# Router scores of tiles 0 to 12 by multiplication on GpSimd and sums on VectorE, in a perceiver block with a mixture of experts

## The chip, the cores and the metric

The kernel runs on one core of a Trainium2 chip. The time is the device time of one launch in microseconds; the figure to compare is the median of several launches. A core has five engines that run side by side, each through its own list of instructions in order: TensorE (PE; its weight loads are listed apart as PEld), VectorE (DVE), ScalarE (ACT), GpSimd (POOL) and SyncE (SP), which here only issues transfers. Where one engine needs what another makes, its instruction waits for a semaphore, and everything behind it on that engine waits too.

## The reference

Three residual stages over x (64 sequences of 32 tokens, 256 wide, all float32). What the change touches is the choice of experts, at the head of the third stage; `Wr` is 8 x 256.

```
x = x + cross_attention(layernorm(x), ctx_512)     # 16 heads of 64, 257 context rows
x = x + self_attention(layernorm(x))               # 4 heads of 64, rotary
x = x + ffn(layernorm(x))

# ffn(x):
scores_BSN = jnp.einsum('bsd,nd->bsn', x, Wr) + br
w_BSN = jax.nn.softmax(scores_BSN, axis=-1)
_, idx_BSK = jax.lax.top_k(scores_BSN + biases_N, 2)
val_BSK = jnp.take_along_axis(w_BSN, idx_BSK, axis=-1)
val_BSK = val_BSK / jnp.sum(val_BSK, axis=-1, keepdims=True)
# each token then goes through its two experts of eight:
# silu(x @ Wl1[:, :512]) * (x @ Wl1[:, 512:]) @ Wl2, weighted by val_BSK
```

## The kernel before

The 2048 tokens are 16 tiles of 128 tokens, and a tile is four sequences of 32. A tile lies with its tokens on the 128 partitions.

**The main loop** goes over the 64 (tile, sequence) pairs. One turn transposes the softmax weights of the present sequence (`tp`, L332), forms the scores of the next sequence in four groups (`s`, L309), and mixes the context (`pa`, L342). Each group of scores gets a maximum on VectorE (`nmx`, L313) and an exponential on ScalarE (L314); after every second group VectorE takes reciprocals (L319) and scales the two groups in place (L321). The scaled weights (`pr`) are what the next turn's `tp` reads. Three PSUM buffers hold the `s` groups.

**Steps in between.** Everything else of a tile is a Python generator that is advanced at six places of a turn, by a table of eight rows: four rows (one for each sequence) for even tiles and four for odd ones. "ahead" advances the queries of later tiles, "near" and "far" the generator `rest` (L528) of the tile before and of the one before that. `rest` runs through output projection, self-attention, a layernorm that writes `xr` (L535), and the router `route` (L470). It has 13 steps: six "near" and, one tile later, seven "far". What is still left of "far" at the end of a tile's fourth row is run off there.

The places of a row are: after the first `tp`; after two score groups; after the second `tp` and the third group; after the fourth group, two places in a row; after the mix. I call the four rows of a tile its first to fourth row.

**The router.** Its first step puts the token number into the last column of `xr` (L472, GpSimd), transposes `xr` in two halves on TensorE (`trr`, L191) and copies the result to SBUF on ScalarE (`xrT`, L192). Its second multiplies with `wr_sb` on TensorE (`pr`, L478, eight columns) and then runs a chain of small VectorE instructions: add the bias (`rsc`, L480), find the two largest (L484 to L488), mark them (`rtwo`, `rboth`, L491 to L495), and form the weights (L497 to L506). Its third counts on TensorE where each token goes in its expert's list (`pk`, L510, from `rboth` and `seen`), forms the slots on VectorE (L513 to L519), and GpSimd scatters `xr` to the list in DRAM (L521, twice). In the trace the PSUM product of the router and the softmax weights of the cross-attention both carry the name `pr`; the line tells them apart.

**Order.** SyncE and TensorE run in the order of the program (`manual_schedule`). VectorE, ScalarE and GpSimd are put in order by the framework's scheduler at compile time; `tc.keep_in_program_order` pins an instruction behind the one that precedes it in the program on its engine.

**Buffers.** The pool `xp` holds, by tags, `xg` (5 buffers: rows gathered for an expert block, and `none`, the zeros that first clear the lists), `y` (4) and `bxT` (2), all used by the expert blocks from tile 15 on. The `xr`, `xaT` and `xrT` tiles have two buffers each in the pool `wk`. PSUM tag `a` has three banks, used by the router's transposition, product and count and by most other products.

**After the loop** the routed tokens go through blocks of 128 for one expert each: six early blocks begin while tiles 14 and 15 finish (L703), the others run with weights streamed in (L732). That part begins at about 640 us.

Of the kernel before, what the change touches and what calls it, by code (L numbers as in the profile page):

```python
# [9 lines left out]
FP = mybir.dt.float32  # L10
U32 = mybir.dt.uint32
AF = mybir.ActivationFunctionType
ALU = mybir.AluOpType
AX = mybir.AxisListType
PSUM = bass.MemoryType.PSUM

P = 128
D = 256
TOK = 2048
NT = TOK // P  # L20
# [9 lines left out]
NE = 8  # L30
# [20 lines left out]
def block_kernel(  # L51
# [13 lines left out]
    awo: bass.AP,  # L65
    abo: bass.AP,
    freq: bass.AP,
    wr_t: bass.AP,
    br: bass.AP,
    bias_n: bass.AP,  # L70
# [4 lines left out]
    nc = tc.nc  # L75
# [19 lines left out]
    def load(dst, src):  # L95
        nc.sync.dma_start(out=dst, in_=src)
# [10 lines left out]
    def pool(name, bufs):  # L107
        return ctx.enter_context(tc.tile_pool(name=name, bufs=bufs))
# [35 lines left out]
    wr_sb = const.tile([P, 2, NE], FP, name="wr_sb")  # L144
    br_bc = const.tile([P, NE], FP, name="br_bc")
# [17 lines left out]
    wk = pool("wk", 2)  # L163
    sm = pool("sm", 4)
    xp = pool("xp", 3)
    tb = pool("tb", 1)

    def bank(shape, name):
        return ps.tile([P] + shape, FP, tag="a", name=name)
# [17 lines left out]
    def transposed(dst, src, n, name):  # L187

        pt = bank([n, P], f"tr{name}")
        for k in range(n):  # L190
            nc.tensor.transpose(pt[:, k, :], src[:, k * P : (k + 1) * P], ident)  # L191
        nc.scalar.copy(dst, pt)  # L192
# [277 lines left out]
    def route(t, xr):  # L470

        nc.gpsimd.tensor_copy(xr[:, RW - 1 : RW], token[:, t : t + 1])  # L472
        xT = wk.tile([P, 2, P], FP, tag="xrT", name=f"xrT{t}")
        transposed(xT, xr, 2, f"r{t}")
        yield
        pr = bank([NE], f"pr{t}")
        for k in range(2):
            nc.tensor.matmul(pr, xT[:, k, :], wr_sb[:, k, :], start=(k == 0), stop=(k == 1))  # L478
        sc = sm.tile([P, NE], FP, tag="rsc", name=f"rsc{t}")
        nc.vector.tensor_tensor(sc, pr, br_bc, ALU.add)  # L480
        sel = sm.tile([P, NE], FP, tag="rsel", name=f"rsel{t}")
        nc.vector.tensor_tensor(sel, sc, bn_bc, ALU.add)
        top = sm.tile([P, 8], FP, tag="rtop", name=f"rtop{t}")
        nc.vector.max(top, sel)  # L484
        idx = sm.tile([P, 8], U32, tag="ridx", name=f"ridx{t}")
        nc.vector.max_index(idx, top, sel)
        idf = sm.tile([P, 2, 1], FP, tag="ridf", name=f"ridf{t}")
        nc.vector.tensor_copy(idf[:, :, 0], idx[:, 0:2])  # L488

        two = sm.tile([P, 2, NE], FP, tag="rtwo", name=f"rtwo{t}")  # L490
        nc.vector.tensor_tensor(  # L491
            two, expert_id2, idf.to_broadcast([P, 2, NE]), ALU.is_equal
        )
        both = sm.tile([P, NE], FP, tag="rboth", name=f"rboth{t}")
        nc.vector.tensor_tensor(both, two[:, 0, :], two[:, 1, :], ALU.add)  # L495
        nmx = sm.tile([P, 1], FP, tag="rnmx", name=f"rnmx{t}")
        nc.vector.tensor_reduce(nmx, sc, AX.X, ALU.max, negate=True)  # L497
        ex = sm.tile([P, NE], FP, tag="rex", name=f"rex{t}")
        nc.scalar.activation(ex, sc, AF.Exp, bias=nmx)
        nc.vector.tensor_tensor(ex, ex, both, ALU.mult)  # L500
        tot = sm.tile([P, 1], FP, tag="rtot", name=f"rtot{t}")
        nc.vector.tensor_reduce(tot, ex, AX.X, ALU.add)
        inv = sm.tile([P, 1], FP, tag="rinv", name=f"rinv{t}")
        nc.vector.reciprocal(inv, tot)
        ew = xr[:, D : D + NE]
        nc.vector.tensor_scalar(ew, ex, inv, None, ALU.mult)  # L506
        yield

        pk = bank([NE], f"pk{t}")
        nc.tensor.matmul(pk, before, both, start=True, stop=False)  # L510
        nc.tensor.matmul(pk, ones, seen, start=False, stop=True)
        at = sm.tile([P, 1, NE], FP, tag="rat", name=f"rat{t}")
        nc.vector.tensor_tensor(at[:, 0, :], pk, region[:, 0, :], ALU.add)  # L513
        nc.vector.tensor_tensor(seen, seen, both, ALU.add)
        nc.vector.tensor_tensor(two, two, at.to_broadcast([P, 2, NE]), ALU.mult)
        slot = sm.tile([P, 2], FP, tag="rslot", name=f"rslot{t}")
        nc.vector.tensor_reduce(slot, two, AX.X, ALU.add)
        slots = sm.tile([P, 2], U32, tag="rslots", name=f"rslots{t}")
        nc.vector.tensor_copy(slots, slot)  # L519
        for k in range(2):  # L520
            nc.gpsimd.indirect_dma_start(  # L521
                out=routed[:, :],
                out_offset=bass.IndirectOffsetOnAxis(ap=slots[:, k : k + 1], axis=0),
                in_=xr,
                in_offset=None,
            )

    def rest(t, cT, lastT, ut):  # L528

        yield from cross_output(t, cT, lastT, ut)  # L530
        xn = normed(t, "s")
        yield
        yield from self_attention(t, xn)
        xr = wk.tile([P, RW], FP, tag="xr", name=f"xr{t}")
        normed(t, "r", xr[:, 0:D])  # L535
        yield
        yield from route(t, xr)
# [265 lines left out]
    def rotary_tables():  # L803
# [72 lines left out]
        ("", "far", "ahead", "near", "far", ""),  # L876
        ("near", "far", "", "near", "far", ""),
        ("ahead", "far", "ahead", "near", "far", "ahead"),
        ("near", "", "ahead", "near", "", "far"),
        ("", "far", "ahead", "near", "far", ""),  # L880
        ("near", "far", "", "near", "far", ""),
        ("ahead", "far", "ahead", "near", "far", "ahead"),
        ("", "", "near", "near", "", "far"),
    )
    kvs, probs = {0: context0}, {}
    seqs = [(t, b) for t in range(NT) for b in range(4)]
# [80 lines left out]
    for n, (t, b) in enumerate(seqs):  # L967
# [31 lines left out]
        pr, pts = probs.pop((t, b)), []  # L999
# [175 lines left out]
```

## Time and profile before

| | us |
|---|---|
| median of 3 launches (809.91 to 810.59) | 810.36 |
| the profiled launch, its own time | 811.05 |
| its span, first to last instruction | 809.3 |
| granted TensorE clock, mean | 0.994 |

Busy time in four stretches of the span, in us:

| stretch | length | PE | DVE | ACT | POOL |
|---|---|---|---|---|---|
| 60 to 100 | 40 | 38.6 | 28.7 | 20.7 | 2.9 |
| 100 to 580 | 480 | 471.5 | 332.4 | 258.3 | 69.1 |
| 580 to 640 | 60 | 55.5 | 39.3 | 25.6 | 17.3 |
| 640 to 809 | 169 | 157.8 | 63.6 | 42.3 | 46.7 |

Rows of the trace that bear on the change (durations of one instruction):

| line, engine | what | shape | ns |
|---|---|---|---|
| L191 PE | `trr`, 2 per tile | 128x128 | 273 |
| L192 ACT | `xrT` copy | 128x256 | 368 |
| L478 PE | `pr`, 4 per tile | 128x8 | 256 |
| L350 POOL | addition of two SBUF tiles | 128x256 | 722 |
| L313 DVE | maximum, from PSUM | 128x257 to 128x1 | 421 |
| L321 DVE | scale, SBUF to SBUF | 128x256 | 350 |
| L497 DVE | maximum, from SBUF | 128x8 to 128x1 | 153 |

How to read it: a page's busy time counts an instruction from start to end, and instructions overlap in an engine's pipe, above all on TensorE; what an instruction costs its engine is better seen from the start of one to the start of the next. An idle time is listed with the instruction that ended it. In a line of the timeline the columns are start, duration, engine, source line, operation, output<-inputs, shapes, count, and in brackets the idle time ahead of it and what released it.

### The profile page before, as it was taken

The page shows a single profiled execution, that of the slowest core. Times are in us where ns is not written, and L with a number is a line of the kernel's source. Part 1 is how long each engine was busy: PE and PEld are TensorE (multiplying, and loading weights), DVE is VectorE, ACT ScalarE, POOL GpSimd, SP SyncE. Part 2 cuts the span into 40 slices and gives each one's busy share as a digit, 9 for nine tenths or more (in the row PEclk, how much of TensorE's full clock was granted, in tenths as well). Part 3 has the DMA queues.
Part 4 walks back from the last instruction along what each step waited for, and adds up shares of the span by engine and source line. Part 5 has one row for each costly group of instructions (what it writes and reads, how often), then busy time and mean ns, then how long its engine had stood idle before and what let it go on. Part 6 is the DMA issues. An engine that isn't in the chain of part 4 may idle for free. (4 is left out here: it accounts for less than half of the span.)

```text
span 809.3 us, 15134 instructions
## 1 busy us (share of the span) xinstructions
PE 778.6 (96%) x5212; PEld 612.5 (76%) x5212; DVE 496.9 (61%) x2045; ACT 378.3 (47%) x1078; POOL 143.7 (18%) x195
## 2 busy tenths in 40 slices
PE   8899999999999999999999999999998999999994
PEld 7576777677767767777767777676677899999994
DVE  4657666766686677677677766768665734334332
ACT  3564555556465555556554555555435322222220
POOL 3001011120201011111101110121123313333332
PEclk9999999999999999999999999999999999999998
DMA  9440202021020202022020102020441495356321
GB/s 306 140 112 1 66 11 67 11 89 51 27 79 11 67 10 80 10 75 65 27 66 11 66 11 67 14 73 15 163 162 34 114 398 144 54 139 210 60 41 21
DMA packets 32735, 64.14 MB, mean 79 GB/s; under 512 B 5328, under 2 KB 23632, under 8 KB 31120
## 3 DMA queue, kind: packets, MB, share of 16 engines
q1 hardware_dynamic: 26128, 54.08, 19.8%
q0 software_dynamic: 6528, 9.06, 6.2%
q8 instruction: 43, 0.70, 0.4%
q14 instruction: 36, 0.29, 0.1%
HBM read 87.54 MB, written 13.16 MB: 124 GB/s over the span
## 5 line engine op out<-in xcount | busy, mean ns | idle before, releaser
L314 ACT ACTIVATE pr<-s,nmx 128x257 f32<-128x257 f32 x256 | 121.7, 479 | 110.1 <-DVE nmx L313 101.9
L313 DVE TENSOR_REDUCE nmx<-s 128x1 f32<-128x257 f32 x256 | 105.8, 421 | 70.3 <-PE s L309 69.7
L309 PE MATMUL s<-kv,q 128*128 128x257 f32 x512 | 142.8, 387 | 1.6 <-ACT pr L314 1.4
L342 PE MATMUL pa<-pt,kv 128*128 128x512 f32 x256 | 123.3, 604 | 5.3 <-ACT ov L366 5.3
L309 PEld LDWEIGHTS s<-kv,q 128*128 128x128 f32 x512 | 89.1, 192 | 16.1 <-ACT pt L336 3.0
L332 PEld LDWEIGHTS tp<-ident,pr 128*128 128x128 f32 x512 | 61.5, 144 | 30.4 <-issue 15.7
L321 DVE TENSOR_SCALAR pr<-pr,inv 128x256 f32<-128x256 f32 x256 | 82.3, 363 | 3.3
L521 POOL DMA_INDIRECT routed<-xr,rslots x32 | 32.9, 1027 | 283.6 <-DVE lastT L1006 215.9
L332 PE MATMUL tp<-ident,pr 128*128 128x128 f32 x512 | 80.2, 278 | 1.6 <-DVE pr L321 1.6
L345 ACT COPY cT<-pa 128x512 f32<-128x512 f32 x64 | 37.5, 585 | 89.3 <-PE pa L342 89.3
L336 ACT COPY pt<-tp 128x512 f32<-128x512 f32 x128 | 75.4, 590 | 6.3 <-PE tp L332 6.0
L342 PEld LDWEIGHTS pa<-pt,kv 128*128 128x128 f32 x256 | 46.1, 190 | 39.8 <-issue 28.3
L695 POOL DMA_INDIRECT out_x<-y_late,to_late x28 | 43.5, 1555 | 107.3 <-DMA out_x<-y_late,to_late 33.5
L285 PE MATMUL pqh<-xqT,xwq_sb 128*128 128x256 f32 x256 | 60.8, 381 | 0.8 <-ACT xqT L192 0.8
L375 PE MATMUL po<-xwo_sb,ov 128*128 128x256 f32 x256 | 60.3, 379 | 0.0
L375 PEld LDWEIGHTS po<-xwo_sb,ov 128*128 128x128 f32 x256 | 48.6, 190 | 6.6
L285 PEld LDWEIGHTS pqh<-xqT,xwq_sb 128*128 128x128 f32 x256 | 47.4, 190 | 7.9 <-ACT xqT L192 1.5
L314 ACT ACTIVATION_READ_ACCUMULATOR pr<-s,nmx 128x1 f32 x256 | 51.7, 202 | 0.0
L319 DVE RECIPROCAL inv<-sums 128x2 f32<-128x2 f32 x128 | 20.5, 160 | 44.3 <-ACT pr L314 44.0
L631 ACT COPY bxT_late<-pxT_late 128x256 f32<-128x256 f32 x28 | 10.4, 372 | 73.1 <-PE pxT_late L629 73.1
L390 PE MATMUL pqkv<-awqkv_sb,xaT 128*128 128x512 f32 (+1 forms) x128 | 43.9, 486 | 0.0
L350 POOL TENSOR_TENSOR xb<-x,xbo_bc 128x256 f32<-128x256 f32 x16 | 11.6, 726 | 165.8 <-issue 117.2
(259 smaller groups left out, 1284.0 us busy)
## 6 DMA issues: line engine op xcount, KB each, us to landing
lane<-in_wall SPq DMA_DIRECT2D x24, 1028.0 KB
lane<-in_wall SPq DMA_DIRECT2D x24, 640.0 KB
lane2a<-in_wall SPq DMA_DIRECT2D x10, 1028.0 KB
kv<-in_ctx_t SPq DMA_DIRECT2D x16, 514.0 KB
kv<-in_ctx_a SPq DMA_DIRECT2D x16, 512.0 KB
lane2b<-in_wall SPq DMA_DIRECT2D x10, 640.0 KB
xg_late<-routed SPq DMA_DIRECT2D x28, 132.5 KB
x<-in_x SPq DMA_DIRECT2D x16, 128.0 KB
```

The costliest lines, as they stand in the source:

```text
L285: nc.tensor.matmul(pq[:, mm, :], xwq_sb[:, k, m * P : (m + 1) * P], xqT[:, k, :], start=(k == 0), stop=(k == 1),)
L309: nc.tensor.matmul(s, qb[:, g * P : (g + 1) * P], kvT[:, b, :], start=True, stop=True)
L313: nc.vector.tensor_reduce(nmx, s, AX.X, ALU.max, negate=True)
L314: nc.scalar.activation(pr[:, g, :], s, AF.Exp, bias=nmx, accum_out=sums[:, g : g + 1])
L321: nc.vector.tensor_scalar(pr[:, i, :ML], pr[:, i, :ML], inv[:, i : i + 1], None, ALU.mult)
L332: nc.tensor.transpose(tp[:, g * P : (g + 1) * P], pr[:, g, j * P : (j + 1) * P], ident)
L336: nc.scalar.copy(pt, tp)
L342: nc.tensor.matmul(pa, kvA[:, b, j, :], pts[j], start=(j == 0), stop=(j == MC - 1))
L345: nc.scalar.copy(cT[:, :, b, :], pa.rearrange("p (h n) -> p h n", n=SEQ))
L375: nc.tensor.matmul(po, ov[:, m, :], xwo_sb[:, m, :], start=False, stop=(m == XH // 2 - 1))
L390: nc.tensor.matmul(pq, xaT[:, k, :], awqkv_sb[:, k, lo:hi], start=(k == 0), stop=(k == 1))
L695: nc.gpsimd.indirect_dma_start(out=out[:, :], out_offset=bass.IndirectOffsetOnAxis(ap=self.to[:, b : b + 1], axis=0), in_=y, in_offset=Non ...
```

## The change

For tiles 0 to 12 (`t < NT - 3`) the router no longer uses TensorE for the scores. The eight rows of `Wr` are loaded once at the start, each spread over all 128 partitions (`wr_rows`; 128 KB each, eight transfers on SyncE's queue behind the other constants). They lie in buffers of the tags `y` and `bxT`, which the expert blocks need only later, and in two new ones. For each expert GpSimd multiplies `xr` with the expert's row, and VectorE sums the product over its 256 columns. This goes in two halves of four experts with a step's end between: the first "far" step issues four products, the second four sums and the next four products, the third the other four sums and the chain from `rsc` on. The sums are pinned in program order; the products use the five `xg` buffers. The router thus has one more step (14 in `rest`), and the two rows of the table that had only one "far" get a second.

Tiles 13, 14 and 15 keep transposition and product; their `xrT` now shares the buffers of the tag `xaT`.

```diff
+    wr_rows = []
+    for e in range(NE):
+        tag, bufs = (("y", 4), ("bxT", 2), ("gates_wr", 2))[(e > 3) + (e > 5)]
+        wr_rows.append(xp.tile([P, D], FP, tag=tag, bufs=bufs, name=f"wr_row{e}"))
+        load(wr_rows[e], wr[e, :].partition_broadcast(P))
...
     def route(t, xr):
 
         nc.gpsimd.tensor_copy(xr[:, RW - 1 : RW], token[:, t : t + 1])
-        xT = wk.tile([P, 2, P], FP, tag="xrT", name=f"xrT{t}")
-        transposed(xT, xr, 2, f"r{t}")
-        yield
-        pr = bank([NE], f"pr{t}")
-        for k in range(2):
-            nc.tensor.matmul(pr, xT[:, k, :], wr_sb[:, k, :], start=(k == 0), stop=(k == 1))
         sc = sm.tile([P, NE], FP, tag="rsc", name=f"rsc{t}")
-        nc.vector.tensor_tensor(sc, pr, br_bc, ALU.add)
+        if t < NT - 3:
+
+            sums = sm.tile([P, NE], FP, tag="rsums", name=f"rsums{t}")
+            for half in range(2):
+                four = range(NE // 2 * half, NE // 2 * (half + 1))
+                prods = {}
+                for e in four:
+                    prods[e] = xp.tile([P, D], FP, tag="xg", bufs=5, name=f"rprod{t}_{e}")
+                    nc.gpsimd.tensor_tensor(prods[e], xr[:, 0:D], wr_rows[e], ALU.mult)
+                yield
+                for e in four:
+                    tc.keep_in_program_order(
+                        nc.vector.tensor_reduce(sums[:, e : e + 1], prods[e], AX.X, ALU.add)
+                    )
+            nc.vector.tensor_tensor(sc, sums, br_bc, ALU.add)
+        else:
+            xT = wk.tile([P, 2, P], FP, tag="xaT", name=f"xrT{t}")
+            transposed(xT, xr, 2, f"r{t}")
+            yield
...
+            nc.vector.tensor_tensor(sc, pr, br_bc, ALU.add)
...
-        ("near", "", "ahead", "near", "", "far"),
+        ("near", "far", "ahead", "near", "", "far"),
...
-        ("", "", "near", "near", "", "far"),
+        ("", "far", "near", "near", "", "far"),
```

More of the change, by code (lines that the diff above doesn't have):

```diff
@@ L67, in block_kernel @@
     freq: bass.AP,
+    wr: bass.AP,
     wr_t: bass.AP,
@@ L472, in route @@
         nc.gpsimd.tensor_copy(xr[:, RW - 1 : RW], token[:, t : t + 1])
-        xT = wk.tile([P, 2, P], FP, tag="xrT", name=f"xrT{t}")
-        transposed(xT, xr, 2, f"r{t}")
-        yield
-        pr = bank([NE], f"pr{t}")
-        for k in range(2):
-            nc.tensor.matmul(pr, xT[:, k, :], wr_sb[:, k, :], start=(k == 0), stop=(k == 1))
-        sc = sm.tile([P, NE], FP, tag="rsc", name=f"rsc{t}")
-        nc.vector.tensor_tensor(sc, pr, br_bc, ALU.add)
+        sc = sm.tile([P, NE], FP, tag="rsc", name=f"rsc{t}")
+        if t < NT - 3:
[16 more added lines that the diff above has]
+            yield
+            pr = bank([NE], f"pr{t}")
+            for k in range(2):
+                nc.tensor.matmul(
+                    pr, xT[:, k, :], wr_sb[:, k, :], start=(k == 0), stop=(k == 1)
+                )
+            nc.vector.tensor_tensor(sc, pr, br_bc, ALU.add)
         sel = sm.tile([P, NE], FP, tag="rsel", name=f"rsel{t}")
@@ L1150 @@
         "freq": a["L0_attn_nrope_freq"],
+        "wr": a["L0_ffn_Wr"],
         "wr_t": a["L0_ffn_Wr"].T,
```

## The prediction

> **What bounds the kernel now.** I read the busy rows and the forty slices first, then what TensorE waits for in the steady part (100 to 580 us), then the timeline around one router, and last the busy time of each row of steps.
>
> ```profile
> PE 778.6 (96%) x5212; PEld 612.5 (76%) x5212; DVE 496.9 (61%) x2045; ACT 378.3 (47%) x1078; POOL 143.7 (18%) x195
> ...
> PE   8899999999999999999999999999998999999994
> DVE  4657666766686677677677766768665734334332
> ```
>
> TensorE is the bound: 9 in nearly every slice, while VectorE stands at 6 to 7 and GpSimd, in its own row, at 0 to 2 until the last third. In the steady part TensorE's waits, by releaser (us in all, times, longest), are small:
>
> ```profile
> PE pa L342 <- ACT ov L366: 4.9, 13, 0.4
> PE trr L191 <- DVE xr L184: 1.6, 2, 0.8
> ```
>
> With two more of 1.0 us each (the second is pr <- q, five times 0.2) that is 8.5 us in 480. So work taken off TensorE is time gained, as long as no new wait arises; and TensorE runs in order, so each new wait is lost whole. The question is how much router work goes, and how late VectorE becomes.
>
> **What goes from TensorE.** An even tile (start and duration in us; "trr" is the router's transposition, "pr" its product):
>
> ```profile
> 182.63 0.38 PE L191 MATMUL trr<-ident,xr 128*128 128x128 f32 x2
> 182.85 0.60 PE L332 MATMUL tp<-ident,pr 128*128 128x128 f32 x4
> ...
> 186.10 0.51 PE L478 MATMUL pr<-wr_sb,xrT 128*128 128x8 f32 x4
> 186.47 1.96 PE L342 MATMUL pa<-pt,kv 128*128 128x512 f32 x4
> ```
>
> Matmuls overlap, so I go from start to start: 182.63 to 182.85 is 0.22 us, 186.10 to 186.47 is 0.37, together 0.59. In the odd tile after it, trr takes 220.24 to 220.46, 0.22, and pr 223.61 to 224.07, 0.46, with 0.20 of idle before it (for a VectorE copy that frees its bank): 0.88. Thirteen routers change (tiles 0 to 12, seven even, six odd): 7 x 0.59 + 6 x 0.88 = 9.4 us. If nothing else moved, the median of 810.4 would become 801.0. ScalarE also loses a copy (L192, 0.37) per tile, 4.8 us in all, off the path.
>
> **What is added.** Eight products per tile on GpSimd. The nearest row is L350, the same shape from two SBUF tiles: 0.72, and two back to back 1.46, so 0.73 each, 5.8 us a tile, 76 us in all. GpSimd goes from 143.7 to about 220 us, 27%. The first four can start when xr is there (181.87) and end by 184.9; their sums are issued behind the row's last scores, about 188. A fifth fits the free buffer; the other three wait for one sum each and end near 191, before the second four sums can begin (195). Behind them in GpSimd's order stand the two scatters, which before left only at 201.3. No wait from there, if no product is longer than 1.2 us.
>
> Eight sums on VectorE, 128x256 from SBUF; none is in the trace. Below: two reductions over 257 elements from PSUM together in 0.75 (220.38), 0.33 from start to start. Above: 0.43, the same pair fed one by one (0.86). Four sums are then 3 x 0.33 + 0.42 = 1.41 us, at most 1.72. I take 1.41, as all four inputs are ready. Over 13 tiles 37 to 45 us.
>
> Eight loads of 128 KB at the start, each of one row given to all partitions: SyncE's issue of the like xbo_bc took 0.43, so 3.5 to 4 us behind bn_bc (18.72). What slides is the zeroing of the scatter buffer, and the second context, issued at 26.0 and first read near 50: 20 us of cover, cost nothing.
>
> The other shapes are free: one more "far" step in each second half-table keeps pace with one more yield (14 steps in place of 13). The last three routers only change the name of a buffer.
>
> **Where it meets the path: the fourth row of steps.** The scores used to be done in the third row (rsc at 186.65), and both picks (rboth, 188.46 + 0.12 = 188.58) lay nine microseconds ahead of pk, which counts them on TensorE. Now the second four sums stand in the fourth row, pinned behind the scale of its first two score groups, and everything from rsc to rboth follows them. What that scale and pk stand at today:
>
> ```profile
> 195.39 0.62 DVE L321 TENSOR_SCALAR pr<-pr,inv 128x256 f32<-128x256 f32 x2
> ...
> 197.86 0.62 DVE L321 TENSOR_SCALAR pr<-pr,inv 128x256 f32<-128x256 f32 x2
> 198.12 0.28 PE L510 MATMUL pk<-rboth,before 128*128 128x8 f32 x2
> ...
> 198.48 0.63 PE L332 MATMUL tp<-ident,pr 128*128 128x128 f32 x4
> ```
>
> The last scale ends at 198.48, just when tp, which reads it, starts: there is no slack here. On this clock less 0.59: the pin opens at 196.01 - 0.59 = 195.42; four sums to 196.83; rsc to rboth took 1.93 with a scale pair (0.61) in between, so 1.32: 198.15. pk is due at 198.12 - 0.59 = 197.53: late 0.62, and 0.42 more if the last maximum (nmx, 196.60) goes in between: 1.04. Behind pk on TensorE stand the next sequence's tp and all that follows; behind the sums on VectorE that nmx, and ScalarE's exponential waits for it. The scale: with nmx after the sums at 196.83 in place of 196.60 - 0.59 = 196.01, plus some of the small instructions, 0.8 to 1.1 late. I take 0.95, less 0.59 gained: +0.36 per even tile.
>
> The odd fourth row is 7.3 us long. VectorE's busy time there and in the even one (columns: span, then PE, PEld, DVE):
>
> ```profile
> 189.40:198.40 9.00, 9.00 (x42) 6.49 (x41) 5.36 (x17) 4.34 (x13) 0.00 (x0) 1.00 0.00 1
> 227.00:234.30 7.30, 7.30 (x34) 4.99 (x33) 5.45 (x18) 3.77 (x12) 0.00 (x0) 1.00 0.00 0
> ```
>
> To 5.45 come 1.41 of sums and some 1.6 of router: 8.5 in 7.3. About 1.2 of rotary and mask work can slide into the next row, but that one has 7.33 of 9.00 already. From the pin (230.62) to the scale's end (234.36) VectorE is idle for 1.0 today, and 2.4 comes in (1.41, and eight small ones at about 0.13 net): 1.4 late, less 0.88: +0.5. Sum: 7 x 0.36 + 6 x 0.5 = 5.5 us. The rotary behind (L401 to L405) is then up to 0.1 late for its transposition: 1.3. Together +6, so 816 for the median. (The profiled run was 811.05, its span 809.3, and 1.75 lies around it; I add to the median.)
>
> **The shared port.** GpSimd's products hold up the scales:
>
> ```profile
> 18.94 1.46 POOL L350 TENSOR_TENSOR xb<-x,xbo_bc 128x256 f32<-128x256 f32 x2 [10.27 <-DMA xbo_bc<-in_xbo]
> ...
> 19.40 1.15 DVE L321 TENSOR_SCALAR pr<-pr,inv 128x256 f32<-128x256 f32 x2
> ```
>
> Under two GpSimd additions the pair took 1.15, elsewhere 0.62: 0.53 lost. One or two pairs a tile meet products, 0.5 to 1.1 us, in the third row, where the last scale ends at 188.21 and tp starts at 189.43: 1.2 of cover, and the router's small work has left. So 0; without the cover 13 x 0.53 = 7 us. The Trainium skill, "SBUF — State Buffer", section "Who interferes with whom", says that GpSimd and a VectorE instruction in a two-port mode hold one port pair in turn, whole instructions long, and that a tensor_reduce never takes it. The row agrees for the scales; by the rule the sums are not slowed, and if they were, by 0.5 for each four, the sum would be 13 us worse. "GPSIMD Engine Reference", section 4.1, advises against elementwise work there as about twice as slow; here 0.72 against VectorE's 0.42, hidden as long as GpSimd has nothing urgent.
>
> **Rivals.** (1) The backlog: as above, 816; own range 811 to 822; 0.42. (2) VectorE hides it: the scores would have to start 1 us earlier than the pin allows today, by ScalarE doing the second exponential of the row before the copy of pt (0.57) that stands ahead of it, and small work yielding to the scales. Speaking for it: VectorE would be only 67% busy. All hidden gives 801, half (0.5 a tile) 807; 0.36. (3) VectorE's fixed order puts sums and router behind the fourth row's last scale (197.89): rboth at 197.89 + 1.41 + 1.32 = 200.6, pk 3.1 late, less 0.59, 2.5 a tile, 33 us: 843; for half the tiles 827. It decides where the compiler believes the products later than they are; against it, they end some 4 us earlier; 0.14. (4) Gain and wait cancel, or the freed 0.7 reappears as another wait: 810; 0.08.
>
> **The numbers.** Within 0.2%, 1.6 us, is about what a measurement tells from no change. Faster 0.36 (case 2), same 0.08, slower 0.56 (1 and 3). Range 801 (all hidden) to 827 (case 3 in half the tiles).
>
> **What would show it.** pk and the next tp waiting for rboth or pr, 0.5 to 1.1 us in each changed tile, right; no such wait and a total near 801, wrong. Sums at 0.33 from start to start, products at 0.73. Wrong too if products end later than their sums are due, or if the third row, not the fourth, holds the new wait.

## The result, and the profile after

The changed kernel takes 828.11 us (median of 5, 827.2 to 828.72) beside 809.91 before (median of 5, 808.56 to 810.59): a ratio of 1.0226, 95% interval 1.0212 to 1.024, so 18.2 us slower. The profiled launch took 828.05, its span 826.3.

The busy row of the page and the group of the products (busy us and mean ns of one, then the idle time ahead of them and what ended it), of the changed kernel:

```profile
PE 776.8 (94%) x5134; PEld 603.7 (73%) x5134; DVE 531.3 (64%) x2149; ACT 373.9 (45%) x1065; POOL 217.6 (26%) x299
...
L490 POOL TENSOR_TENSOR rprod<-xr,wr_row 128x256 f32<-128x256 f32 x104 | 73.5, 739 | 37.3 <-DVE rsums L494 34.2
```

TensorE has 1.8 us less to do by this count, VectorE 34 more, GpSimd 74 more. TensorE's waits in its steady part (100 to 595 us) show where the time went:

```profile
PE pk L536 <- DVE rboth L521: 12.9, 13, 3.1
PE pa L350 <- DVE q L285: 6.5, 6, 1.2
```

Both are new: 12.9 us before pk, in all thirteen changed tiles, and 6.5 us in six places where the context product waits for VectorE's copy of q (before, the longest wait for this copy was 0.2). Both come from VectorE being late.

**Row by row.** The kernel repeats the same work, so the loss can be located. I take the start of each sequence's first `pa` from TensorE's timeline and measure from one to the next. B runs from a tile's first row to its second, C from the second to the third, D from the third to the fourth, E from the fourth to the next tile's first. C holds the router's old work on TensorE, E holds pk and the next tp. Means over four even and four odd tiles (tiles 4 to 11), in us; starts are read to 0.01, so a mean can be off by as much:

| | even B | C | D | E | odd B | C | D | E |
|---|---|---|---|---|---|---|---|---|
| before | 9.92 | 8.59 | 9.93 | 9.17 | 9.92 | 8.58 | 8.21 | 8.35 |
| after, less before | 0.00 | -0.59 | -0.07 | +1.66 | 0.00 | +0.29 | +0.02 | +0.86 |

Tile 14, in which the router of tile 12 runs, stands apart: C, D and E are -0.47, +0.60 and +5.39. From the first `pa` of the loop to the last one it is 18.6 us more, which is the whole loss. What comes ahead of the loop and behind it is not longer, and the eight new loads cost nothing that shows: of two kernels among the experiments below, t11, which has them, comes to its first `pa` at 27.7 us, and sums_only, which has not, at 27.9.

The even E, in the timeline of the changed kernel (the two sums of four are one line, x4):

```profile
195.35 0.62 DVE L329 TENSOR_SCALAR pr<-pr,inv 128x256 f32<-128x256 f32 x2
...
195.88 1.39 DVE L494 TENSOR_REDUCE rsums<-rprod 128x1 f32<-128x256 f32 x4
...
197.19 0.41 DVE L321 TENSOR_REDUCE nmx<-s 128x1 f32<-128x257 f32 x1
...
197.52 0.16 DVE L496 TENSOR_TENSOR rsc<-rsums,br_bc 128x8 f32<-128x8 f32 x1
...
198.46 0.35 DVE L329 TENSOR_SCALAR pr<-pr,inv 128x256 f32<-128x256 f32 x1
...
198.81 0.35 DVE L329 TENSOR_SCALAR pr<-pr,inv 128x256 f32<-128x256 f32 x1
199.08 0.16 DVE L521 TENSOR_TENSOR rboth<-rtwo 128x8 f32<-128x8 f32 x1
...
199.29 0.39 PE L536 MATMUL pk<-rboth,before 128*128 128x8 f32 x2 [1.06 <-DVE rboth L521]
...
199.76 0.63 PE L340 MATMUL tp<-ident,pr 128*128 128x128 f32 x4
```

The pin opens at 195.9, the four sums end at 197.3, the last maximum goes ahead of rsc, and the reciprocal and both scales go between rsc and rboth. pk waits 1.06 us on TensorE's row until 199.29, and the last scale ends at 199.16, so that tp could not have run much earlier either.

The odd C:

```profile
221.55 3.57 POOL L490 TENSOR_TENSOR rprod<-xr,wr_row 128x256 f32<-128x256 f32 x5
...
224.18 1.10 DVE L329 TENSOR_SCALAR pr<-pr,inv 128x256 f32<-128x256 f32 x2
...
225.20 0.68 DVE L285 COPY q<-pq 128x512 f32<-128x512 f32 x1
...
225.93 1.98 PE L350 MATMUL pa<-pt,kv 128*128 128x512 f32 x4 [1.18 <-DVE q L285]
```

Five products run on GpSimd from 221.55 to 225.12. The pair of scales at 224.18 takes 1.10 in place of 0.61; the copy of q behind it ends at 225.88 and `pa`, which takes the bank that this copy frees, waits 1.18 us.

The end of tile 14:

```profile
566.08 1.39 DVE L494 TENSOR_REDUCE rsums<-rprod 128x1 f32<-128x256 f32 x4
...
567.50 0.17 DVE L496 TENSOR_TENSOR rsc<-rsums,br_bc 128x8 f32<-128x8 f32 x1
...
569.59 0.16 DVE L521 TENSOR_TENSOR rboth<-rtwo 128x8 f32<-128x8 f32 x1
...
569.80 0.60 PE L536 MATMUL pk<-rboth,before 128*128 128x8 f32 x2 [3.11 <-DVE rboth L521]
...
571.23 0.59 PE L572 MATMUL pc_early<-seen,ones 128*128 128x8 f32 x2 [0.40 <-DVE seen L540]
```

Here rsc to rboth takes 2.2 us, as the rotary instructions go in between, pk waits 3.11 us and the count for the early blocks follows at once. From the row's first `pa` to pk it is 4.99 us, 3.28 more than before. Behind pk lies a second loss: from 569.5 to 576.4 us the granted TensorE clock was 0.51. The same four transpositions behind the count, in the changed kernel and in chain_late, an experiment below that also waits 0.40 for the count:

```profile
571.67 1.09 PE L340 MATMUL tp<-ident,pr 128*128 128x128 f32 x4
```
```profile
561.63 0.63 PE L332 MATMUL tp<-ident,pr 128*128 128x128 f32 x4
```

From pk to the next `pa` the changed kernel takes 9.99 us, chain_late 7.25. So some 2.7 us of this row are the lower clock, an estimate from these two kernels. The loop of the kernel before has no such stretch.

### The profile page after: what moved, and what is told of

The parts are those of the page before. It is cut to its first block, busy times and chain, and to the rows that moved or that the text cites. A ratio compares the mean times of both kernels' runs of the same rounds, so it can differ in the third digit from the quotient of the medians.

```text
span 826.3 us, 15143 instructions
## 1 busy us (share of the span) xinstructions
PE 776.8 (94%) x5134; PEld 603.7 (73%) x5134; DVE 531.3 (64%) x2149; ACT 373.9 (45%) x1065; POOL 217.6 (26%) x299
## 5 line engine op out<-in xcount | busy, mean ns | idle before, releaser
L329 DVE TENSOR_SCALAR pr<-pr,inv 128x256 f32<-128x256 f32 x256 | 89.6, 388 | 3.7
L490 POOL TENSOR_TENSOR rprod<-xr,wr_row 128x256 f32<-128x256 f32 x104 | 73.5, 739 | 37.3 <-DVE rsums L494 34.2
L350 PEld LDWEIGHTS pa<-pt,kv 128*128 128x128 f32 x256 | 46.0, 190 | 47.9 <-issue 27.1
```

Of the source, the lines that this page charges most:

```text
L329: nc.vector.tensor_scalar(pr[:, i, :ML], pr[:, i, :ML], inv[:, i : i + 1], None, ALU.mult)
L350: nc.tensor.matmul(pa, kvA[:, b, j, :], pts[j], start=(j == 0), stop=(j == MC - 1))
L490: nc.gpsimd.tensor_tensor(prods[e], xr[:, 0:D], wr_rows[e], ALU.mult)
```

## The experiments

My theory was that VectorE is late in two places, each by its own cause: in the fourth row by the sums and the chain, in the odd third row by GpSimd's products. The rivals put all of it on one of these parts, on pk's place, or on the order of the PSUM banks; what theory 1, 2 or 3 stands for in a run is said in its expectation. Times are medians, each with the ratio to the kernel before on the same chip; row numbers are as in the table above. The kernel before stood at 810.58, 809.67 and 810.75 beside the three groups of runs.

**t11: tile 12 left as it was.**

```diff
-        if t < NT - 3:
+        if t < NT - 4:
```

> The changed kernel, but tile 12 keeps transposition and product on TensorE (tiles 0 to 11 changed). In the changed kernel the rows from the third row of tile 14 to the first of tile 15 are 5.5 us longer than before, with pk waiting 3.1 us for rboth. Theory 1 (this loss belongs to tile 14 alone, where no query work covers the fourth row and the early blocks' count follows at once): about 822.6 us, and tile 14 as long as before. Theory 2 (whichever router is last pays): the loss moves to tile 13, 826 us or more.

820.57 us, ratio 1.0144 (1.0115 to 1.0173). C, D and E of tile 14 are -0.04, +0.26 and -1.27, and tile 13 is no longer than in the changed kernel (E +0.83 beside +0.82). Theory 1: one router of thirteen made tile 14 longer by 6.6 us (5.52 and 1.05), of 7.5 in the median. The stretch of low clock is part of it: t11 has none in its loop. The even tiles' E is also lower, +1.38 in place of +1.66, though their own steps are the same; why stays open.

**products_only: GpSimd's products alone.** The kernel before, with five products of xr and a constant tile in the router's first step.

```diff
+        if t < NT - 3:
+            for e in range(5):
+                prod = xp.tile([P, D], FP, tag="xg", bufs=5, name=f"rprod{t}_{e}")
+                nc.gpsimd.tensor_tensor(prod, xr[:, 0:D], xbo_bc, ALU.mult)
```

> The kernel before, with five products (xr times a constant 256-wide tile) added on GpSimd at the router's first step of tiles 0 to 12, read by nobody; scores stay on TensorE. Theory 1 (the odd tiles' third row is lengthened by GpSimd's products, which hold up VectorE's scales and the copy of q behind them): odd third rows about 1 us longer than before, even ones unchanged, in all 5 to 7 us: 815 to 817. Theory 2 (the new wait of pa for q comes from the changed turn of the PSUM banks after two allocations are gone): no row changes, 810.

817.48 us, ratio 1.0091 (1.0066 to 1.0115). Odd C is +1.04 in tiles 3 to 11 and +0.50 in tile 13, tile 14 is 0.34 longer, and every other row is within 0.01. In its timeline:

```profile
220.73 0.94 DVE L184 TENSOR_SCALAR xnq<-x,mvq,rstdq 128x256 f32<-128x256 f32 x1
220.79 3.53 POOL L478 TENSOR_TENSOR rprod<-xr,xbo_bc 128x256 f32<-128x256 f32 x5
...
223.62 1.11 DVE L321 TENSOR_SCALAR pr<-pr,inv 128x256 f32<-128x256 f32 x2
...
224.65 0.68 DVE L277 COPY q<-pq 128x512 f32<-128x512 f32 x1
...
225.39 0.61 PE L482 MATMUL pr<-wr_sb,xrT 128*128 128x8 f32 x4 [1.24 <-DVE q L277]
```

And in the kernel before:

```profile
219.98 0.41 DVE L184 TENSOR_SCALAR xnq<-x,mvq,rstdq 128x256 f32<-128x256 f32 x1
...
222.34 0.61 DVE L321 TENSOR_SCALAR pr<-pr,inv 128x256 f32<-128x256 f32 x2
...
223.61 0.61 PE L478 MATMUL pr<-wr_sb,xrT 128*128 128x8 f32 x4 [0.20 <-DVE q L277]
```

The same pattern as in the changed kernel, with nothing else changed. Beside the products a subtraction takes 0.53 us more and the scale pair 0.50 more, q is late by both, and TensorE waits 1.24 for it in place of 0.20, which is the 1.04. Theory 1; the turn of the PSUM banks is not needed to explain it.

**sums_only: VectorE's sums alone.** The kernel before with the table of the change and eight pinned sums over a constant.

```diff
...
+            for e in range(4):
+                tc.keep_in_program_order(
+                    nc.vector.tensor_reduce(sums[:, e : e + 1], xbo_bc, AX.X, ALU.add)
+                )
         pr = bank([NE], f"pr{t}")
...
         yield
+        if t < NT - 3:
+            for e in range(4, 8):
+                tc.keep_in_program_order(
+                    nc.vector.tensor_reduce(sums[:, e : e + 1], xbo_bc, AX.X, ALU.add)
+                )
+            yield
```

> The kernel before, with the eight pinned sums added on VectorE where the changed kernel has them (four behind the third row's last scale, four in the fourth row behind the first scale pair), over a constant tile and read by nobody; scores on TensorE, router chain in the third row as before, one more step in the table. Theory 1 (the four sums alone put the last maximum and scale back by 0.6 to 0.7 us, the rest of the loss is the chain ahead of pk): fourth rows 0.5 to 0.7 us longer, pk without a wait, in all 7 to 9 us: 817 to 819. Theory 2 (VectorE has room once the chain is away): 811 to 813. Theory 3 (any four sums there cost what the whole change costs): 823 or more.

820.99 us, ratio 1.0144 (1.0115 to 1.0174). E is +0.47 in even and +1.08 in odd tiles, C and D within 0.01. pk waits nowhere; in the odd tiles TensorE now waits for the scale, and in the even ones the wait falls inside the group of transpositions that reads it, which takes 1.07 us in place of 0.63 (197.67):

```profile
PE tp L332 <- DVE pr L321: 3.8, 6, 0.7
```

Between theories 1 and 3: the mechanism of 1, with odd tiles at nearly twice its price. The sums alone, without a chain behind them, cost 10.4 us; the 18.2 of the whole change are what is left after TensorE's gain.

**chain_late: the chain alone in the fourth row.** TensorE's scores, copied to SBUF, and rsc pinned where the change has it, with the table of the change.

```diff
...
+            prs = sm.tile([P, NE], FP, tag="rprs", name=f"rprs{t}")
+            nc.scalar.copy(prs, pr)
+            yield
+            tc.keep_in_program_order(nc.vector.tensor_tensor(sc, prs, br_bc, ALU.add))
```

> The kernel before with TensorE's scores (copied to SBUF by ScalarE in the third row), but the router chain from rsc to the weights pinned in the fourth row behind the first scale pair, where the changed kernel has it; no products, no sums. Theory 1 (the chain alone has time there: 1.3 to 1.9 us behind 196.0 is before 198.1, when pk is due; only sums and chain one behind the other are late): no wait at pk, fourth rows at most 0.3 us longer, 810 to 813. Theory 2 (the chain ahead of pk costs what it costs in the changed kernel beyond the sums, 0.9 us in even tiles): 815 or more.

815.24 us, ratio 1.0063 (1.0039 to 1.0088), beside 810.75. E +0.39 and +0.15, tile 14's E +1.14; pk waits in tile 14 alone, 1.60 us. The time is in theory 2's range, but its 0.9 in even tiles is not there; the rows are nearer to theory 1, too low for even tiles, and tiles 14 and 15 make 1.9 of the loop's 5.1. Sums 0.47 and chain 0.39 make 0.86 in even tiles, where both together cost 1.38 to 1.74: one behind the other is dearer than each alone. In odd tiles it is the other way round, 1.08 and 0.15 beside 0.86, in a row that follows a loss in C; why stays open.

**count_late: pk taken out of the fourth row.** As t11, with the router's last step at the end of the next tile's first row.

```diff
...
-        ("", "far", "ahead", "near", "far", ""),
+        ("", "far", "ahead", "near", "far", "left"),
...
-        ("near", "far", "ahead", "near", "", "far"),
+        ("near", "far", "ahead", "near", "", ""),
...
-            for _ in work["far"]:
-                pass
+            work["left"] = work["far"]
```

> As t11, and the router's last step (pk and the scatter) comes at the end of the first row of the next tile instead of the end of the fourth row. Theory 1 (pk waiting for rboth is what ends TensorE's wait in the fourth row; the scale pair is late by a smaller amount, 0.65 us in even tiles, some 0.5 in odd ones): each even fourth row gains about 0.9 us, each odd one 0.5, in all 8 us against t11: about 814. Theory 2 (VectorE's work in the fourth row as a whole is what is late, and tp waits for the scales nearly as long as pk did): at most 3 us gained, 819 to 822.

823.13 us, ratio 1.0167 (1.0144 to 1.019). Against t11, E falls by 0.62 (even) and 0.19 (odd), and B rises by 0.40, which is pk itself in its new place: no gain. No wait at pk is left, and TensorE waits at tp in its stead (the releasers named are the neighbours of the scales in VectorE's order):

```profile
PE tp L340 <- DVE rtwo L517: 3.1, 6, 0.5
PE tp L340 <- DVE rboth L521: 2.2, 6, 0.4
```

Theory 2, though the time is above its range: pk was only the first to arrive, VectorE's work as a whole is late. The loops of the two kernels differ by 0.1 us, the medians by 2.6. In the two profiles the rest is 2.0 ahead of the loop and 1.0 behind it. There the granted clock of count_late was 0.5 from 23.7 to 27.1 us and from 634.7 to 638.1, that of t11 full; whether this is all of it stays open.

**even_only: odd tiles on TensorE.**

```diff
-        if t < NT - 3:
+        if t < NT - 4 and t % 2 == 0:
```

> The changed kernel with only the even tiles 0 to 10 changed, odd tiles and tile 12 on TensorE. Theory 1 (each parity pays by itself: even tiles lose 1.38 in the fourth row and gain 0.67 in the second and third, odd ones lose by GpSimd's products in the third row and by sums and chain in the fourth): odd tiles' rows as before, even ones as in t11; 6 x 0.7 = 4.3 us and some 0.7 at the end: about 815 beside 810.5 before. Theory 2 (the losses are carried from one tile to the next): odd rows still longer by 0.3 us or more, 818.

816.87 us, ratio 1.0081 (1.0055 to 1.0108). Even tiles pay as before (E +1.54), and odd tiles are not free: D +0.39, E -0.05. Their router still has 13 steps, and in the new table its pk comes one place earlier: D grows by pk's time, but E does not shrink by it, since the group of tp waits for the scale there (1.02 us in place of 0.64). So theory 1 missed what the table does to odd tiles, and theory 2's losses carried from tile to tile are not needed. It also means that pk at its old place had filled time in which TensorE would have waited. The same happens once in the changed kernel, in tile 15, D +0.71 (also in t11, sums_only and chain_late, all with the new table; 0.01 in the kernels below, with the old one).

**unpinned: the changed kernel without the pins.**

```diff
-                    tc.keep_in_program_order(
-                        nc.vector.tensor_reduce(sums[:, e : e + 1], prods[e], AX.X, ALU.add)
-                    )
+                    nc.vector.tensor_reduce(sums[:, e : e + 1], prods[e], AX.X, ALU.add)
```

> The changed kernel without the pins on the eight sums, so that the scheduler places them. Theory 1 (it puts them earlier than GpSimd really is, and VectorE waits for products with maxima and scales behind it): 830 or more, with waits of rsums for rprod. Theory 2 (it finds better gaps, since the pin behind the first scale pair is what makes the second four late): 818 to 825.

856.17 us, ratio 1.0575 (1.0546 to 1.0604). VectorE waits for products, and TensorE for VectorE:

```profile
DVE rsums L493 <- POOL rprod L490: 19.5, 58, 0.8
```
```profile
PE s L317 <- DVE rsums L493: 14.3, 7, 2.1
```

C and D are 1.1 to 2.3 us longer, E only 0.2 and 0.0. Theory 1: the scheduler has the products ready earlier than they are. The waits are not all of the 45 us: in eight stretches of the loop, some 37 us together, the granted clock was 0.5.

**early_even and early_all: everything in the third row.** Seven product buffers, all products in the first step, all sums and the chain in the second, the old table; even tiles 0 to 10, or all of 0 to 11.

```diff
...
+            for e in range(NE):
+                prods.append(xp.tile([P, D], FP, tag="xg", bufs=7, name=f"rprod{t}_{e}"))
+                nc.gpsimd.tensor_tensor(prods[e], xr[:, 0:D], wr_rows[e], ALU.mult)
+            yield
+            for e in range(NE):
+                tc.keep_in_program_order(
+                    nc.vector.tensor_reduce(sums[:, e : e + 1], prods[e], AX.X, ALU.add)
+                )
```

> Even tiles 0 to 10 only, and all eight products in the router's first step (seven buffers instead of five), all eight sums and the chain in its second, at the end of the third row, as TensorE's scores were; the table of steps as before. Theory 1 (the loss is sums and chain in the fourth row): fourth rows as before within 0.2 us, third and second 0.67 shorter, 6 x 0.67 = 4 us gained: 806 to 807. Theory 2 (2.8 us of sums at any place of VectorE push the maxima and scales behind them on to TensorE's path): even fourth rows 0.5 us or more longer, 809 to 813.

808.65 us, ratio 0.9993 (0.9973 to 1.0014). Even C -0.59, D -0.08, E +0.33, odd rows unchanged: a loop 2.0 us shorter. Near theory 1, with half of the gain given back in E; in time no difference that can be told.

> As early_even, for all tiles 0 to 11. Theory 1 (in odd tiles GpSimd's products hold up scales and the copy of q, whatever becomes of the sums): odd third rows 0.3 to 1.0 us longer than before, the fourth about as before, even tiles as in early_even: 808 to 813. Theory 2 (the port costs little once sums and chain are out of the fourth row): odd rows shorter than before too, 801 to 804.

816.25 us, ratio 1.008 (1.0049 to 1.0112). Odd C +0.29 and E +0.98: theory 1 for the third row, but a time above its range, as the fourth row pays too: the loop is 4.2 us longer, and 3.2 more lie behind it in the profile. The wait for q is back:

```profile
PE pa L350 <- DVE q L285: 6.5, 6, 1.2
```

**fused_all, split_even and split_all: no GpSimd.** One VectorE instruction multiplies and sums; all eight in the second step, or four in each of the first two.

```diff
...
+            for e in range(NE):
+                if e == NE // 2:
+                    yield
+                prod = xp.tile([P, D], FP, tag="xg", bufs=5, name=f"rprod{t}_{e}")
+                tc.keep_in_program_order(
+                    nc.vector.scalar_tensor_tensor(
+                        prod, xr[:, 0:D], 1.0, wr_rows[e], ALU.mult, ALU.mult,
+                        accum_out=sums[:, e : e + 1],
+                    )
+                )
```

(split; fused_all has the `yield` ahead of the loop.)

> As early_all, but with no products on GpSimd: each expert's multiplication and sum is one VectorE instruction with an accumulator, eight of them pinned at the head of the router's second step, each 0.42 us and a short read of the accumulator, some 4 us. Theory 1 (without GpSimd no scale is held up in the odd third row, but 4 us on VectorE reach into the fourth row): odd third rows 0.5 us or more shorter than before, fourth rows 0.5 to 2 us longer, in all 810 to 822. Theory 2 (VectorE has room in the gap ahead of the fourth row's products): 801 to 805.

810.58 us, ratio 1.0001 (0.9987 to 1.0016). Odd C is -0.65, where the products had made it +0.29; E +0.38 and +0.58 take most of the gain back: the loop is 1.7 us shorter, but in the profile 2.1 more lie behind it. Theory 1, at its lower end. The group's busy time and mean:

```profile
L488 DVE SCALAR_TENSOR_TENSOR rprod<-xr,wr_row 128x256 f32<-128x256 f32 x96 | 34.1, 420 | 0.0
...
L488 DVE DVE_READ_ACCUMULATOR rprod<-xr,wr_row 128x1 f32 x96 | 7.9, 82 | 0.0
```

> Even tiles 0 to 10, multiplication and sum fused on VectorE (0.44 us each in fused_all), four pinned in the router's first step and four in its second, no GpSimd, the table as before. Theory 1 (four at a time fit VectorE's gaps in the third row, 1.1 us idle ahead of the last maximum and 1.2 us of slack at the scale): third and second rows 0.67 shorter, fourth within 0.2 of before, 6 x 0.5 to 0.67 = 3 to 4 us gained: 806. Theory 2 (the first four delay the third row's last scale past tp): 809 to 812.

809.09 us, ratio 0.9981 (0.9968 to 0.9995), beside 810.75. Even C -0.59, D -0.08, E +0.30, odd rows as before: the loop is 2.2 us shorter. The direction of theory 1, half its size. It is the only version here whose interval lies below 1, by 1.7 us in 811.

> As split_even for all tiles 0 to 11. Theory 1 (in odd tiles the first four stand ahead of the copy of q, which frees pa's bank, and cost there what GpSimd's hold cost): odd third rows 0 to 1 us longer than before: 806 to 813. Theory 2 (odd tiles gain 0.66 in the third row as in fused_all, and nothing is left for the fourth): 802.

812.95 us, ratio 1.003 (1.0011 to 1.0049). Odd C -0.70, E +0.98: theory 2 for the third row; the first four sums do not hold up q, but the rest reaches into E:

```profile
PE tp L340 <- DVE pr L329: 3.5, 6, 0.6
```

Even tiles gain 0.35 as in split_even, odd ones lose 0.30, and the loop is as long as before (0.1 us shorter). So the 2.2 us of the median lie outside it. In the profile 3.9 more lie behind the loop, with a wait of 2.24 for `xr` in place of 1.43 and the granted clock at 0.5 from 623.8 to 627.2. Of its ten launches the one with the highest clock, 0.996, took 809.03. What makes the end longer stays open.

## Why the prediction was right or wrong

The side was right, and so was the place of the largest loss, the fourth row with pk waiting for rboth. The size was not: 18.2 us in place of the likeliest case's 6, just above the range. Three steps failed: the shared port was put at nothing, the lateness in the fourth row too low, and the last router was priced like the others.

**What held.** TensorE gains 0.59 in an even tile's C (and 0.08 in D), as worked out from start to start; without GpSimd the odd one gains 0.65 to 0.70, where 0.88 was put: the 0.20 of idle counted in it stays, now ahead of `pa` (fused_all, five times 0.2). Four sums take 1.39 (1.41 put), a product 0.73, the loads nothing. No sum waited for a product. The place was mainly the fourth row, and pk waited for rboth there in every changed tile.

**"So 0" for the shared port failed,** in the odd tiles. I had taken the next tp as the consumer of a late scale, with 1.2 us of cover. The consumer that matters stands elsewhere on VectorE: the copy of q behind the scales, which frees the PSUM bank that TensorE takes next. It had no cover at all: the view of waits already showed that wait, five times 0.2. Priced by products_only it is 1.04 us per odd tile, a subtraction held by 0.53 and a scale pair by 0.50. In the third row it turned a gain of about 0.65 into a loss of 0.29. The prediction had named a new wait in the third row as a sign of being wrong: 6.5 us of new waits are there, beside 12.9 in the fourth.

**"+0.36 per even tile" was too small.** From the pin to the end of rboth I put 2.73 to 3.15 us; it took 3.36 (195.88 to 199.24), because the maximum, the reciprocal and both scales went in between. E rose by 1.38 to 1.74 where 0.95 was put. In the tile shown pk starts 1.22 us later behind the row's first `pa` than before, tp 1.33, the next `pa` 1.61, so some 0.3 is lost behind tp. The runs show why a single late step does not measure it: take pk away and tp waits for the scale (count_late); take the chain away and the scale is still late (sums_only). The right sum was VectorE's whole work between the pin and tp.

**"+0.5" per odd tile** counted the backlog, 1.4, against a gain of 0.88. E rose by 0.86, less than put, but the gain was gone with the port: +1.17 in all. (The 7.33 of 9.00 put for the row behind it belong to 198.40 to 207.40, behind an even tile; from 234.30 to 243.30 VectorE is busy for 7.57.)

**Tile 12 was not priced.** I multiplied two steady rows by thirteen. The last changed router runs in tile 14, where no query work is left to cover the fourth row and the early blocks' count follows pk: 5.5 us of the 18.2. Of its last row's 5.39, 3.28 come up to pk; the rest lies behind it, in the stretch of low clock, for which the prediction had no term. The table's second "far", called free, costs 0.7 in tile 15.

Together, by rows: even tiles 5.8, odd ones 5.8 and 0.8 for the last, tile 14 5.5, tile 15 0.7 make 18.6, as much as the loop. The forecast had 6.8 in the same terms. Of the rivals, the backlog was the right one. VectorE hiding everything never occurred in any version, and the order that puts all sums behind the row's last scale did not occur either.

## What to carry to other kernels

Ahead of moving work to an engine with idle time, list which of its instructions another engine waits for with no cover, in every row of the schedule, and add the new work ahead of each of those; a mean load of two thirds says nothing about it. Price the last repetitions of a loop by themselves, since the work that covers the others may have run out. Look at the granted clock behind each long new wait: in tile 14 the row lost nearly as much there as in the wait. And a multiplication in front of a sum need not be given to another engine: here VectorE did both in one instruction at nearly the price of the sum.

## What the runs showed of the hardware

The fused multiplication and sum over 128x256 took 0.42 us, and 0.08 for reading the accumulator, which overlaps the next one: four in a row take 1.46 us (split_even, 181.79 to 183.25). The sum alone took 0.41 (407 to 415 ns over all 104), four in a row 1.39:

```profile
L494 DVE TENSOR_REDUCE rsums<-rprod x104: 407/410/415, 113.5 to 567.1; 128x1 f32<-128x256 f32 x104
```

So GpSimd's 73.5 us of products saved VectorE almost nothing. Under them a scale pair took 1.09 to 1.62 us in place of 0.62, and a subtraction with two scalars per token (L192, SBUF to SBUF) 0.93 in place of 0.41 (221.50 in the changed kernel), but no sum was longer, though 39 of the 104 ran beside products (407 to 414 ns; some of those at 227.64). That agrees with the rule of the Trainium skill named in the prediction ("SBUF — State Buffer", section "Who interferes with whom"): a scale is held while GpSimd works, a tensor_reduce is not.

The granted clock is full throughout the loop in all kernels but two. In the changed kernel it was 0.51 from 569.5 to 576.4 us, from the end of a TensorE wait of 3.11. In unpinned it was 0.5 in eight stretches of 3.4 or 6.8 us; seven of them begin within 2 us of the end of a TensorE wait of 1.97 us or more, and twelve waits were that long. In the other loops no wait was longer than 1.6 us. That such waits bring the low clock on is not shown: no experiment varies them alone.
